# A convolution stack's two ends: W's first tile laid out whole, and a last layer with seven held tiles in four column tiles

## The chip, the cores and the metric

The kernel runs on one core of a Trainium2 chip. TensorE (PE in the profile, its weight loads PEld) multiplies matrices into PSUM; VectorE (DVE), ScalarE (ACT) and GpSimd (POOL) work on data in PSUM and SBUF; SyncE (SP) only issues DMAs. ScalarE and GpSimd issue DMAs too, each on a queue of its own. Each engine runs its instructions in the order written and waits on semaphores where it needs another's result. The metric is the device time of one execution in microseconds, and the profile shows one execution in detail.

## The reference, cut to what matters

The input x has 4 images of 32 x 32 pixels with 16 channels, in float32. Four layers follow each other, each with a residual: `x = x + layer(group_norm(x))`, with groups of two channels.

Layers 0 to 2 have this form, each with its own weights M, Wp and G:

```python
first = jnp.einsum('ijpq,bpqc->bijc', M2, inputs)
shifted = conv3x3(inputs, K)             # K is G: 32*32*16 output channels
shifted = shifted.reshape(b, h, w, h, w, f)
diff = jax.nn.relu(inputs[:, :, :, None, None, :] - shifted)
second = jnp.einsum('ijpq,bpqijc->bijc', W2, diff)
return first - second
```

For every one of the 1024 target positions there is a 3 x 3 convolution with its own weights over the whole image; its result is subtracted from the image, clipped at zero, and summed over the image with weights W.

Layer 3 is a convolution with the impulse response of a rational filter:

```python
H_truncated = jnp.fft.rfft2(b, s=(l1, l2)) / jnp.fft.rfft2(a, s=(l1, l2))
h_truncated = jnp.fft.irfft2(H_truncated, s=(l1, l2))
...
y = irfft2(einsum(rfft2(x), h0 + rfft2(h_truncated[0])))[..., :l1, :l2, :]
```

## The kernel before, in words

**Layers 0 to 2** (`conv_layer`). The 1024 positions are packed into 128 blocks of 8 positions x 16 channels, so that a block is 128 columns of weights. For one block and one of the four batches TensorE runs 12 matmuls (L470) into one PSUM pair: the taps lie in three weight tiles (`ga`, `gb`, `gn`) against three image copies `ims[a]`, one set for batches 0 and 1 (a = 0) and one for batches 2 and 3. VectorE then clips the result, multiplies it with a row of W and sums it, in one instruction (L478). Four PSUM pairs rotate, so TensorE can be at most four blocks ahead of VectorE.

G comes in chunks of 8 blocks (`load_g`), two 64-row loads each for `ga` and `gb` and one broadcast load for the last tap; `prepare_g` subtracts an identity on GpSimd (L398), casts on ScalarE (L402) and takes a remainder on VectorE (L405). W comes in tiles of two blocks, 1 MB each (`load_w`, L420): W's eight rows are each copied to 16 partitions, by a broadcast in the DMA. Six W tiles rotate, and a tile is fetched four tiles ahead of its use, on SyncE's queue. The first term is computed on the side (`first_term`): M's tiles (`load_m`) come from a pool `mp` of four buffers that is kept through the whole kernel.

**The start** loads three raw image copies for each half of the batches (`load_first`) and a first quarter of G's first chunk (`halves[0]`, two blocks) on three queues. The other three quarters (`halves[1]`) are loaded by GpSimd's queue. On SyncE's queue come, in this order, the copies for batches 0 and 1, the small G loads, two copies for batches 2 and 3, W's first tile in two halves (`load_w(2)`), W's second tile, and G's second chunk. `first_images` then normalises the copies: ScalarE subtracts the mean (L176), GpSimd clears borders (L194), ScalarE and VectorE scale (L180, L198 to L205).

**Steps on the side.** `step()` is called after every block and moves each generator in `todo` by one yield; this is how the norms are spread over the matmuls. `group_norm` yields once after the sums, once after the sums of squares are started, and once more, and only then has TensorE add the sums over the groups (L102).

**Layer 3.** While the earlier layers run, `impulse_response` writes the filter to DRAM (`hd`). `load_toeplitz` reads from it one tile of four rows of taps, with eight DMAs of 160 KB, half on SyncE's and half on ScalarE's queue. There are eight such tiles, used in the order 1, 7, 6, 5, 4, 3, 2, 0. Five are loaded during layer 2 into five buffers (`TB = 5`); the last three are loaded each into a buffer that layer 3 has just finished with. Tiles 1 and 0 are multiplied with 128 columns of the normalised image `y3` at a time. Tiles 7 to 2 are multiplied in groups of four matmuls with 32 columns each, a column tile for each, since a part of the output needs only some of the taps (`slots`). Results go to one PSUM bank for the part that lies in place (`po`) and three banks (`other`) for parts that belong to another block of rows. `po` shares a PSUM pair with `other[1]`, and `other[2]` with `other[3]`. VectorE adds the three banks to the residual `xo` at L722, after tiles 6, 4 and 2, and `po` at the end (L762). The residual itself is copied (L704), transposed on TensorE (L707) and copied back (L711) between the last norm and the first matmul of layer 3 (L747).

Of the kernel before, what the change touches and what calls it, by code (L numbers as in the profile page):

```python
# [37 lines left out]
P = 128  # L38
# [16 lines left out]
def conv_stack_kernel(ctx, tc, x, raw, M, W, G, den, num, h0, cst, dft, one, idp, idq, out):  # L55
# [10 lines left out]
    mp = ctx.enter_context(tc.tile_pool(name="mp", bufs=4))  # L66
# [233 lines left out]
    def load_m(layer, pm):  # L300
        mt = mp.tile([P, 2, 512], F32, tag="mt", name="mt")
        nc.sync.dma_start(out=mt.rearrange("k h n -> k (h n)"), in_=M[layer][:, pm])
        return mt

    def first_term(layer, xt):

        mts = [load_m(layer, 0)]
        yield
        py = small_psum()
        for b in range(B):  # L310
            nc.tensor.transpose(py[:, bass.ts(b, P)], yc[b // 2][:, b % 2, :], ident)  # L311
        yt = work.tile([P, 8, B, C], F32, tag="yt", name="yt")
        nc.vector.tensor_copy(yt, py.rearrange("k (b p c) -> k p b c", b=B, p=8))
        for pm in range(1, 4):
            mts.append(load_m(layer, pm))
            yield
        for _ in range(GC - 4):
            yield
        ft = work.tile([P, 2, 8, S], F32, tag="ft", name="ft")
        for part in range(2):  # L320
            pf = small_psum()
            for k in range(4):
                for h in range(2):
                    nc.tensor.matmul(  # L324
                        pf[64 * h : 64 * h + 64],
                        lhsT=yt[:, 4 * part + k].rearrange("k b c -> k (b c)"),
                        rhs=mts[k][:, h, :],
                        start=(k == 0),
                        stop=(k == 3),
                    )  # L330
            pv = pf.rearrange("k (cc p q) -> k cc p q", cc=2, p=8)
            if part == 0:
                nc.scalar.copy(ft, pv)
                mts = []
                for pm in range(4, 8):
                    yield
                    mts.append(load_m(layer, pm))
                for _ in range(GC - 4):
                    yield
            else:  # L340
                nc.vector.tensor_tensor(ft, ft, pv, ALU.add)  # L341
# [67 lines left out]
    def load_w(parts=1):  # L409
# [6 lines left out]
        src = W[layer][cc, :, q : q + 2, :].rearrange("p k m -> p (k m)")  # L416
        wts.append(wt)
        n = 2 * S * S // parts
        for k in range(parts):
            nc.sync.dma_start(  # L420
                out=wt.rearrange("p k m -> p (k m)")[:, bass.ts(k, n)],
                in_=src[:, bass.ts(k, n)].unsqueeze(1).to_broadcast([8, C, n]),
            )
            yield
# [10 lines left out]
    def conv_layer(layer, xt, finish, side=()):  # L435
# [15 lines left out]
        for job, (blks, batches) in enumerate(jobs):  # L451
            pairs = layer and job < 2, job >= len(jobs) - 2
            for k, blk in enumerate(blks):
                if any(pairs):

                    if k in ((4, 6) if job != len(jobs) - 2 else (0, 2)):
                        list(load_w())
                elif k % 2 == 0:
                    list(load_w())
                if k == (3 if job == 0 else 1):  # L460
                    list(load_g(layer, blk // GC + 1))
                if (job or not layer) and k == 6:
                    list(prepare_g(layer, blk // GC + 1))
                wt = wts[64 * layer + blk // 2][:, blk % 2, :]
# [163 lines left out]
    def load_toeplitz(k):  # L628

        t = tp.tile([P, TQ, C, PITCH], F32, tag="t", name="t")  # L630
        ts.append(t)
        n = TQ * C * PITCH
        for p in range(8):
            src = hd[8 + k * n - p :]
            (nc.sync, nc.scalar)[p % 2].dma_start(
                out=t[p * C : (p + 1) * C].rearrange("i q j r -> i (q j r)"),
# [221 lines left out]
```

## Time and profile before

| What | us |
|---|---|
| median of 3 runs | 3146.19 |
| lowest and highest | 3145.56, 3148.74 |
| profiled execution, its own time | 3146.99 |
| span of the profiled execution | 3145.2 |
| TensorE busy in it | 3112.3 |
| VectorE busy in it | 2069.8 |

All times in the profile are counted from the start of the span. Busy time of TensorE is modelled, since its matmuls overlap. One matmul of float32 is shown as two instructions, so that the 224 matmuls of layer 3 stand as 448. The profile's chain of waits runs back from the last instruction to whatever released it. "granted clock" is the share of TensorE's clock that a throttle let through; in this execution it was half for a part of the start (from 23.2 to 26.6 us) and from 3084.9 to 3095.2 us.

### The profile page before, as it was taken

How to read it: one execution, taken by the hardware profiler on the slowest of the kernel's cores; microseconds unless marked ns; L12 is line 12 of the kernel's file. 1: busy time of each engine (PE TensorE's matmuls, PEld its weight loads, DVE VectorE, ACT ScalarE, POOL GpSimd, SP SyncE). 2: the span in 40 equal slices, each digit the busy share in tenths (PEclk: the TensorE clock that was granted, in tenths of full speed). 3: DMA queues.
4: the chain of work that ended last, by engine and by line, in shares of the span. 5: the costliest groups of instructions: out<-in, count | busy, mean ns of one | idle time of the engine just before them, and what ended most of it. 6: DMA issues, size and time to landing. Idle time of an engine off the chain costs nothing.

```text
span 3145.2 us, 38886 instructions
## 1 busy us (share of the span) xinstructions
PE 3112.3 (99%) x16068; PEld 1563.7 (50%) x16068; DVE 2069.8 (66%) x3318; ACT 82.0 (3%) x107; POOL 235.1 (7%) x262
## 2 busy tenths in 40 slices
PE   7999999999999999999999999999999999999998
PEld 5545554454444554444444444455444444444444
DVE  6666766666667766666666666766666666666662
ACT  1000000000000000000000000000000000000000
POOL 2002320000000100100000000010010000000000
PEclk9999999999999999999999999999999999999999
DMA  7553344433443655433443344266544444444303
GB/s 193 133 129 93 88 108 110 99 88 88 96 99 71 132 142 124 98 88 88 98 97 87 88 98 97 61 137 150 127 101 98 97 114 103 98 99 111 88 14 54
DMA packets 67206, 321.18 MB, mean 102 GB/s; under 512 B 9987, under 2 KB 16901, under 8 KB 41557
## 3 DMA queue, kind: packets, MB, share of 16 engines
q1 hardware_dynamic: 56176, 299.31, 40.1%
q10 hardware_dynamic: 6356, 10.81, 1.8%
q0 software_dynamic: 4496, 8.58, 1.5%
q8 instruction: 126, 2.06, 0.3%
q14 instruction: 52, 0.42, 0.0%
HBM read 313.03 MB, written 5.63 MB: 101 GB/s over the span
## 4 chain that ended last, share of the span: by engine, by line
PE 98%; DMA 2%; DVE 1%; issue 0%; ACT 0%; SPq 0%; ACTq 0%; DVEq 0%
PE pt L470 95%; PE pt L747 1%; DMA t<-hd 1%; DMA w<-in_W_dram 1%; PE pt L324 1%; DVE junk L478 0%; DMA im<-in_raw_dram 0%; PE pt L523 0%; PE pt L566 0%; PE pt L102 0%; PE pt L605 0%; DVE x L493 0%; DVE s L111 0%; PE pt L311 0%; DVE xo L722 0%
## 5 line engine op out<-in xcount | busy, mean ns | idle before, releaser
L478 DVE SCALAR_TENSOR_TENSOR junk<-pt,w 128x1024 f32<-128x1024 f32 x1536 | 1880.8, 1224 | 999.5 <-PE pt L470 976.6
L470 PE MATMUL pt<-im,ga 64*128 64x512 f32 x6144 | 1592.3, 591 | 5.1 <-POOL im L194 2.8
L470 PE MATMUL pt<-im,gb 64*128 64x512 f32 x6144 | 1585.1, 589 | 3.5 <-ACT im L180 3.3
L470 PE MATMUL pt<-im,gn 64*128 64x512 f32 x3072 | 1259.8, 806 | 0.0
L470 PEld LDWEIGHTS pt<-im,gb 64*128 64x128 f32 x6144 | 607.0, 185 | 718.1 <-issue 707.7
L470 PEld LDWEIGHTS pt<-im,ga 64*128 64x128 f32 x6144 | 605.4, 187 | 435.2 <-DVE junk L478 278.0
L470 PEld LDWEIGHTS pt<-im,gn 64*128 64x128 f32 x3072 | 305.3, 186 | 356.6 <-issue 352.7
L398 POOL TENSOR_TENSOR ga<-ga,cs 128x1024 f32<-128x1024 f32 (+2 forms) x49 | 113.6, 2319 | 2129.3 <-DMA ga<-in_G_dram 2080.3
L478 DVE DVE_READ_ACCUMULATOR junk<-pt,w 128x1 f32 x1536 | 127.8, 83 | 0.0
L405 DVE TENSOR_TENSOR gn<-g,gn 32x1024 fp32r<-32x1024 f32 (+2 forms) x98 | 120.7, 1232 | 4.7 <-ACT gn L402 2.6
L402 ACT CAST gn<-g 128x1024 fp32r<-128x1024 f32 (+2 forms) x49 | 50.4, 1029 | 2332.1 <-DMA g<-in_G_dram 2201.0
L747 PE MATMUL pt<-t,y 128*32 128x512 f32 (+4 forms) x448 | 46.6, 440 | 4.8 <-DVE xo L722 2.7
L348 POOL DMA_DIRECT2D fd<-ft x48 | 25.1, 531 | 219.3 <-DVE ft L341 209.7
L747 PEld LDWEIGHTS pt<-t,y 128*32 128x32 f32 (+1 forms) x448 | 24.8, 125 | 26.7 <-issue 19.1
L722 DVE TENSOR_TENSOR xo<-xo,pt 32x512 f32<-32x512 f32 x5 | 3.4, 681 | 40.0 <-PE pt L747 39.9
L324 PE MATMUL pt<-mt,yt 128*64 128x512 f32 x96 | 21.9, 599 | 0.0
L291 POOL DMA_DIRECT2D im<-img x32 | 16.2, 515 | 9.1 <-DMA img<-y 9.1
L544 POOL TENSOR_TENSOR H<-H,d 128x256 f32<-128x256 f32 (+1 forms) x10 | 8.3, 826 | 68.1 <-DVE d L549 67.7
L324 PEld LDWEIGHTS pt<-mt,yt 128*64 128x64 f32 x96 | 6.4, 136 | 13.7 <-issue 9.4
L102 PE MATMUL pt<-s,cs 64*128 64x2 f32 (+1 forms) x28 | 2.9, 266 | 9.2 <-DVE s L111 9.2
L274 POOL COPY e<-y 32x612 f32<-32x612 f32 x4 | 2.8, 694 | 119.2 <-DVE y L273 119.2
L544 POOL TENSOR_TENSOR t<-s 128x256 f32<-128x256 f32 (+1 forms) x15 | 11.3, 756 | 0.0
(83 smaller groups left out, 186.3 us busy)
## 6 DMA issues: line engine op xcount, KB each, us to landing
w<-in_W_dram SPq DMA_DIRECT2D x191, 1024.0 KB
ga<-in_G_dram SPq DMA_DIRECT2D x94, 256.0 KB
gb<-in_G_dram SPq DMA_DIRECT2D x94, 256.0 KB
g<-in_G_dram SPq DMA_DIRECT2D x47, 512.0 KB
mt<-in_M_dram SPq DMA_DIRECT2D x24, 512.0 KB
t<-hd ACTq DMA_DIRECT2D x32, 160.0 KB
t<-hd SPq DMA_DIRECT2D x32, 160.0 KB
im<-img SPq DMA_DIRECT2D x32, 67.5 KB
```

Source lines behind the costliest of these rows:

```text
L102: nc.tensor.matmul(pt[:, h, : s.shape[1]], lhsT=avg[rows], rhs=s[rows], start=True, stop=True)
L291: (nc.sync, nc.scalar, nc.gpsimd)[n % 3].dma_start(out=ims[a][k][at : at + C] .bitcast(F32) .rearrange("c l b cc x -> c l (b cc x)")[:, :, ...
L324: nc.tensor.matmul(pf[64 * h : 64 * h + 64], lhsT=yt[:, 4 * part + k].rearrange("k b c -> k (b c)"), rhs=mts[k][:, h, :], start=(k == 0), ...
L348: nc.gpsimd.dma_start(out=fv[h, cc, b], in_=ft[at : at + C, cc])
L398: nc.gpsimd.tensor_tensor(gv, gv, mid.unsqueeze(1).to_broadcast([P, gv.shape[1], C]), ALU.subtract)
L402: nc.scalar.copy(gn, g9)
L405: nc.vector.tensor_tensor(lo, g9[r : r + 32], lo.bitcast(F32), ALU.subtract)
L470: nc.tensor.matmul(pt[:, half, :], lhsT=w[rows, blk % GC, :], rhs=im[rows, :, b % 2, :, :S], start=n == 0, stop=n == 2,)
L478: nc.vector.scalar_tensor_tensor(junk, pt.rearrange("p h m -> p (h m)"), 0.0, wt, ALU.min, ALU.mult, accum_out=acc[b // 2][:, b % 2, blk : ...
L544: mul = lambda o, u, w: nc.gpsimd.tensor_tensor(o, u, w, ALU.mult)
L722: nc.vector.tensor_tensor(out, out, src, ALU.add)
L747: nc.tensor.matmul(bank[cols].rearrange("n (j r) -> n j r", j=C)[:, :, 8 * cc :], lhsT=y3[:, cc, at : at + width, :].rearrange("p q b -> p ...
```

## The change

It touches both ends of the kernel.

At the start, W's first tile is laid out for all 128 partitions by the host (`w0`) and loaded with one plain DMA, instead of two broadcast DMAs. The load is issued ahead of the rest of G's first chunk, and the `ga` and `gb` loads of that rest move from GpSimd's queue to SyncE's, behind it. Its broadcast load for the last tap stays with GpSimd.

M's pool is opened inside `first_term` and closed after its last matmul, so that its space can be used later in each layer.

In layer 3, seven of the eight tiles are held when it starts: five as before, one in space that M's pool gave back (`tp2`), and one in the buffers of two W tiles that layer 2 no longer needs, loaded from its last job but one on (`late_toeplitz`). Only tile 0 is loaded during layer 3, into the buffer of tile 1. Tiles 1 and 0 are now also multiplied in four column tiles, and `po` has a PSUM pair of its own. VectorE's additions of the three other banks, one for each pair of column tile and block (five), all stand after the last tile but one. The residual's copy, transposes and copy back move into the norm of batches 2 and 3 (`norm3`, a = 1), between its two group sums. In doing so `norm3` takes two steps of `group_norm` itself and drops one of its yields, also for batches 0 and 1.

```diff
-    mp = ctx.enter_context(tc.tile_pool(name="mp", bufs=4))
...
     def first_term(layer, xt):
-        mts = [load_m(layer, 0)]
+        ft = work.tile([P, 2, 8, S], F32, tag="ft", name="ft")
+        with tc.tile_pool(name="mp", bufs=4) as mp:
+            mts = [load_m(mp, layer, 0)]
...
-    def load_w(parts=1):
+    def load_w():
...
+        nc.sync.dma_start(
+            out=wt.rearrange("p k m -> p (k m)"),
+            in_=src.unsqueeze(1).to_broadcast([8, C, 2 * S * S]) if wts else w0,
+        )
         wts.append(wt)
-        n = 2 * S * S // parts
-        for k in range(parts):
-            nc.sync.dma_start(
-                out=wt.rearrange("p k m -> p (k m)")[:, bass.ts(k, n)],
-                in_=src[:, bass.ts(k, n)].unsqueeze(1).to_broadcast([8, C, n]),
-            )
-            yield
...
+                if job == len(jobs) - 2:
+                    next(late, None)
...
-                (halves[1], nc.gpsimd, nc.gpsimd, nc.gpsimd),
+                (halves[1], nc.sync, nc.sync, nc.gpsimd),
...
+        load_w()
         list(loads)
-        list(load_w(2))
         first_images()
-        list(load_w())
+        load_w()
...
     def norm3(a, xt):
-        xc, rstd = yield from group_norm(xt[:, 2 * a : 2 * a + 2])
+        steps = group_norm(xt[:, 2 * a : 2 * a + 2])
+        if a:
+            xr = work.tile([P, 4, S, B], F32, tag="ft", name="xr")
+            nc.scalar.copy(xr, xt.rearrange("p b (cc q) -> p cc q b", q=S))
+        next(steps)
+        yield
+        next(steps)
+        if a:
+            px = small_psum()
+            for cc in range(4):
+                nc.tensor.transpose(
+                    px[:, bass.ts(cc, P)], xr[:, cc].rearrange("p q b -> p (q b)"), ident
+                )
+            nc.scalar.copy(xo, px.rearrange("n (r j) -> n r j", j=C))
+        xc, rstd = yield from steps
...
     def toeplitz():
         for k in order[:TB]:
-            for _ in load_toeplitz(k):
+            for _ in load_toeplitz(k, toeplitz_tile(tp)):
                 yield
                 yield
+        yield from load_toeplitz(order[TB], toeplitz_tile(ctx.enter_context(tc.tile_pool(name="tp2", bufs=1))))
+
+    def late_toeplitz():
+        half = TQ // 2 * C * PITCH
+        parts = []
+        for _ in range(2):
+            wt = wp.tile([P, 2, S * S], F32, tag="w", name="w").rearrange("p k m -> p (k m)")
+            parts.append(wt[:, :half].rearrange("p (q j r) -> p q j r", j=C, r=PITCH))
+        ts.append([part[:, q] for part in parts for q in range(TQ // 2)])
+        yield from load_toeplitz(order[TB + 1], *parts)
...
-    banks = [pair_psum(), pair_psum()]
-    po, other = banks[0][:, 0], {1: banks[0][:, 1], 2: banks[1][:, 0], 3: banks[1][:, 1]}
+    banks = [pair_psum() for _ in range(3)]
+    po, other = banks[0][:, 0], {1: banks[1][:, 0], 2: banks[1][:, 1], 3: banks[2][:, 0]}
...
-        [[(None, None, q)] for q in range(TQ)],
+        [[(t, t, q) for t in range(4)] for q in range(TQ)],
...
-        if n and n + TB - 1 < len(order):
-            list(load_toeplitz(order[n + TB - 1]))
+        if n == 1:
+            list(load_toeplitz(order[-1], toeplitz_tile(tp)))
...
-        if k == 6:
-            add(3, 2, other[3])
-        elif k == 4:
-            add(3, 1, other[3])
-        elif k == 2:
-            for block in range(1, 4):
-                add(block, 0, other[block])
+        if n == len(order) - 2:
+            for tile, block in sorted({m for m in every if m[0] != m[1]}):
+                row = xo[32 * block : 32 * block + 32]
+                src = other[block][32 * tile : 32 * tile + 32].rearrange("n (j r) -> n r j", j=C)
+                nc.vector.tensor_tensor(row, row, src, ALU.add)
...
+        if i == 0:
+            arrays["w0"] = np.repeat(arrays["W0"][0, :, :2].reshape(8, -1), C, axis=0)
```

## The prediction

> **What bounds the kernel now.** I read the page first: TensorE is busy almost all the time, and the chain of work that ended last is 95% convolution matmuls (L470).
>
> ```profile
> span 3145.2 us, 38886 instructions
> PE 3112.3 (99%) x16068; PEld 1563.7 (50%) x16068; DVE 2069.8 (66%) x3318; ACT 82.0 (3%) x107; POOL 235.1 (7%) x262
> PE pt L470 95%; PE pt L747 1%; DMA t<-hd 1%; DMA w<-in_W_dram 1%; PE pt L324 1%; DVE junk L478 0%; DMA im<-in_raw_dram 0%; PE pt L523 0%; PE pt L566 0%; PE pt L102 0%; PE pt L605 0%; DVE x L493 0%; DVE s L111 0%; PE pt L311 0%; DVE xo L722 0%
> ```
>
> Between about 30 and 3082 us a block (one position, one batch) costs TensorE 1.96 us (in the timeline one block's first matmul starts at 3077.81, the next one's at 3079.77) and VectorE 1.32 (1.23 + 0.08). The change leaves those instructions alone, so only the two ends can move. Second, the start, in the timeline and as windows (columns: window, its length, busy us of PE, PEld, DVE, ACT, POOL, then granted PE clock, DMA share, GB/s).
>
> ```profile
> 19.37 1.39 ACT L176 ACTIVATE im<-im,neg 128x544 f32<-128x544 f32 x2 [3.34 <-DMA im<-in_raw_dram]
> 22.30 1.39 ACT L180 ACTIVATE im<-im,rstd 128x544 f32<-128x544 f32 x2 [1.55 <-POOL im L194]
> 23.10 2.08 PE L470 MATMUL pt<-im,gb 64*128 64x512 f32 x4 [3.34 <-ACT im L180]
> 29.11 1.23 DVE L478 SCALAR_TENSOR_TENSOR junk<-pt,w 128x1024 f32<-128x1024 f32 x1 [7.11 <-DMA w<-in_W_dram]
> 30.40 1.13 PE L470 MATMUL pt<-im,ga 64*128 64x512 f32 x4 [2.30 <-DVE junk L478]
> ```
>
> ```profile
> 23.10:28.10 5.00, 4.99 (x16) 2.24 (x16) 0.00 (x0) 0.59 (x1) 1.80 (x1) 0.66 1.05 128
> 28.10:30.40 2.30, 0.00 (x1) 0.01 (x1) 1.23 (x2) 0.83 (x1) 0.00 (x0) 1.00 0.88 119
> 30.40:38.30 7.90, 7.90 (x40) 3.91 (x42) 7.34 (x12) 0.00 (x0) 0.00 (x0) 1.00 0.53 130
> ```
>
> TensorE fills its four PSUM buffers by 28.10 and then stands for 2.30 us, because VectorE cannot empty the first one before half of W's first tile lands at 29.1. One step earlier there is a second gate: batches 2 and 3 wait for the last image copy (landed 19.37), which goes through ScalarE, GpSimd and ScalarE again, and reaches TensorE 3.73 us later, at 23.10. Third, the end, as the chain (start, us, what) and in windows.
>
> ```profile
> 3089.00 1.12 PE pt L707 x4
> 3090.12 11.18 PE pt L747 x32
> ...
> 3114.65 9.15 DMA t<-hd
> 3123.80 0.18 issue
> 3123.98 6.70 PE pt L747 x96
> 3130.68 0.02 issue
> 3130.70 0.68 DVE xo L722
> 3131.38 0.03 issue
> 3131.41 0.69 DVE xo L722
> 3132.10 0.41 issue
> 3132.51 8.88 PE pt L747 x32
> ```
>
> ```profile
> 3106.59:3121.87 15.28, 15.28 (x224) 6.94 (x224) 0.68 (x1) 0.00 (x0) 0.00 (x0) 1.00 1.02 139
> ```
>
> **The change part by part: the start.** W's first tile (1 MB, in two halves) is now one plain 128-row load; the other 6/8 of G's first chunk (four loads of 192 KB) leave GpSimd's queue for SyncE's, behind that tile. (1) The W tile. The row for a broadcast tile is the last window of the start: 130 GB/s at a DMA share of 0.53, about 8 us per MB. The row for plain 128-row loads is the 5 to 10 us window, 321 GB/s: 1.05 MB / 321 = 3.3 us. Ends: 2.5 us (420 GB/s, the best 1.5 us slice of the first 60 us) and 8 us (if nothing is won). It sits on SyncE's queue directly behind the last image copy, so it lands near 19.0 + 3.3 = 22.3 us, at worst 27. (2) VectorE has image work in its order until 22.01, so the first L478 runs at about 22.3 instead of 29.11. (3) What is late next: the image copy, not W. Between 12 and 20 us GpSimd's queue moved 1.06 MB beside it (0.54 + 0.52 in the queue view), the rest of one image and G. The four G loads go away there, but the 384 KB broadcast of G's last taps, issued behind them, moves up and takes their place, so I give the copy 0.4 us only (ends: 1 us later, since broadcasts are the slow loads here, and 2.5 us earlier). TensorE then starts batch 2 at 22.7 and, with the 5.00 us that batches 2 and 3 took at a granted clock of 0.66, reaches the second block at 27.7 instead of 30.40: **-2.7 us**. The low end is -1.3 (copy 1 us later, 30.40 - 29.1). The high end is -5.5: copy 1.2 us earlier and the clock not dropped, so 3.3 us in place of 5.0.
>
> What is behind the moved loads: G's 768 KB at 269 GB/s (the 7.35 to 19.36 window) is 2.9 us, in by 25.2; GpSimd's subtraction (1.80) ends near 27 and TensorE needs it at 27.7 + 4 x 1.96 = 35.5. W's second tile stands behind them: 25.2 + 8 = 33.2, needed by VectorE at 37.5, and TensorE only stands if it is more than three blocks (5.9 us) later still. That cover is why the longer SyncE queue costs nothing; if the second tile took past 43 us, each us beyond is a us lost. GpSimd issues four DMAs fewer (about 0.54 each), which nothing on the path waits for. From there TensorE runs at 1.96 per block to the end, so the lead is kept.
>
> **The middle.** M's tiles now come from a pool opened per layer, whose space later tiles take over. The added waits are on M's readers (L324) and loads, which are over some blocks before: zero. The two more Toeplitz tiles (10 x 128 KB each, 2.6 MB) are loaded in layer 2 by SyncE and ScalarE: one between W tiles up to block 107 or so, one into the buffers of W tiles 58 and 59 after block 119. Queued behind them are the last W tiles, fetched four tiles (63 us) ahead, and ScalarE's cast of the last G chunk. DMA is idle from 2988 to 3066 us (share 0 in that slice of the page), and about 10 us per tile (9.60 and 9.15 in the chain) fits in the 63 us left: zero; ends 0 and +3 (one missed cast).
>
> The norm of batches 0 and 1 loses one step of delay: its second group sums stand one block earlier in TensorE's order. VectorE finishes ss at 3054.41, and sums follow VectorE by 0.14 (3084.12 to 3084.26); TensorE would be there at 3054.03, so it stands 0.5 us, with the restart **+0.6** (ends 0.4 and 0.9).
>
> **The end.** (a) The residual copy (1.08 on ScalarE) and four transposes (1.12) now run inside the last norm. x is ready at 3083.66, so the copy ends at 3084.8 and the transposes at 3085.95; the second sums wait for ss until 3086.42, so they hide, with 0.5 us to spare. The path is then y's end (3089.40) + 0.14: layer 3 starts at 3089.54, not 3090.12. (b) Seven tiles are held, so two of the three loads on the path go; the third is issued after the first tile, takes about 9.5 us, and has six tiles = 48 groups x 0.546 = 26 us of matmuls over it. (c) Tiles 1 and 0 change from 16 wide matmuls to 16 groups of four in column tiles. Rows: 15.28 us for 28 groups (224 instructions), 0.546 per group; wide, 8.88 / 16 = 0.555. So neutral. Ends 0.53 and 0.56. (d) The VectorE additions go to one place beside the last tile (5 x 0.68 = 3.4 under 8.8) and have PSUM tiles of their own, so TensorE's stalls of 0.86, 2.10 and 1.87 us at 3105.7, 3121.9 and 3130.7 all go (4.8 together).
>
> Sum: 80 groups x 0.546 = 43.7, plus the slow clock of the first tile, plus 0.2 to drain. The clock row: 0.77 over the 11.40 us from 3089.9, a loss of 2.6. 3089.54 + 46.5 = 3136.0; last addition at 3136.0 instead of 3141.42: **-5.4**. With +0.6: **-4.8** (ends -2.9 and -6).
>
> [...]
>
> Total -2.7 - 4.8 = -7.5 us. The profiled execution took 3146.99 (span 3145.2 and 1.8 around it), 0.8 above the median of 3146.19; its terms taken from the median give **3138.7 us**.
>
> **Rivals.**
> - A, as above: 3138.7, own range 3136 to 3141.5.
> - B, the start gives twice as much: copy 1 us earlier or the clock kept (for: 28 to 34 us show 1.00 once it is busy; against: TensorE would still be idle about 2.9 us from 19.8). -5.2 - 4.8: 3136.2.
> - C, one end gives little: the last-taps broadcast slows the image copy or W's tile by 2 us and more (for: 128 GB/s while broadcasts ran, from 23 to 28 us). 3141.4; with the end failing in its place, 3143.5.
> - D, slower: four column tiles that stream the very same rows from SBUF at once, as tiles 1 and 0 now do, take turns. In the trace groups share rows in pairs at most; pairs ran at 0.546 like the others, which speaks against it. 32 groups change, so the gain is gone at 0.546 + 7.5/32 = 0.78 us per group, slower by 0.2% at 0.98, and at full turns (2.18) the time is 3138.7 + 52 = 3191.
>
> **How the numbers follow.** A 0.59, B 0.15, C 0.18, D 0.08. A measurement of this kernel tells 0.2% (6.3 us) from no change, so the line is 3139.9. A lies below it three times in four (0.44), B always (0.15), C seldom (0.03): faster 0.62. The rest of A (0.15) and of C (0.15) is the same: 0.30. D is slower: 0.08. The range takes A, B and most of C: 3134.5 to 3143.
>
> **What would show it.** First L478 near 22 us with no wait for W of over 1 us, and block 1 starting near 27.7; the image copy still ending near 19. At the end, no wait for t or for xo from the second tile on, layer 3's matmuls in one run of about 46.5 us with 640 instructions, and all xo additions but one before it ends. Wrong would be: L478 waiting for W's second tile past 43 us, a group of tiles 1 or 0 above 0.6 us, a wait of ScalarE's last casts, or a granted clock below 0.77 for longer than the first tile.

## The result, and the profile after

The changed kernel took 3144.76 us (median of 3145.93, 3146.66, 3136.89 and 3143.59); the kernel before took 3147.06 in the runs beside it. The ratio is 0.9988, with a 95% interval from 0.997 to 1.0006: no difference that this measurement can tell. The forecast was 3138.7 and "faster". Both ends gave what was forecast, as the trace shows, and yet most of it is missing from the total. The profiled execution took 3145.93 with a span of 3144.1, which is 1.1 us below the span of before.

The page of the changed kernel: span, busy times, and the chain that ended last by line.

```profile
span 3144.1 us, 39279 instructions
PE 3113.4 (99%) x16260; PEld 1538.3 (49%) x16260; DVE 2070.0 (66%) x3318; ACT 81.8 (3%) x107; POOL 232.6 (7%) x258
PE pt L470 94%; PE pt L761 1%; DMA g<-in_G_dram 1%; DMA w<-in_W_dram 1%; PE pt L324 1%; DMA im<-in_raw_dram 0%; DVE junk L478 0%; PE pt L523 0%; PE pt L566 0%; PE pt L605 0%; PE pt L101 0%; DVE x L493 0%; DVE s L110 0%; PE pt L312 0%; DVE gn L405 0%
```

The loads of Toeplitz tiles (`t<-hd`) are gone from the chain, and of the additions to `xo` only the last one (0.69 us) is left on it, too short for this list. A load of G (`g<-in_G_dram`) and VectorE's remainder of G's last taps (`gn L405`) have come in. That is the first sign of where the gain went.

**The start.** The timeline of the changed kernel (start, us, engine, line, in brackets the wait before it):

```profile
19.15 1.39 ACT L175 ACTIVATE im<-im,neg 128x544 f32<-128x544 f32 x2 [3.04 <-DMA im<-in_raw_dram]
22.02 1.39 ACT L179 ACTIVATE im<-im,rstd 128x544 f32<-128x544 f32 x2 [1.48 <-POOL im L193]
22.82 1.21 PE L470 MATMUL pt<-im,gb 64*128 64x512 f32 x4 [2.95 <-ACT im L179]
24.25 1.22 DVE L478 SCALAR_TENSOR_TENSOR junk<-pt,w 128x1024 f32<-128x1024 f32 x1 [2.13 <-DMA w<-in_w_dram]
27.65 1.03 PE L470 MATMUL pt<-im,ga 64*128 64x512 f32 x4
```

W's first tile no longer holds TensorE up: the first L478, which still waits 2.13 us for it, runs at 24.25 in place of 29.11, and TensorE goes on to the second block at 27.65 without a gap, where it started at 30.40 before. (A block from here on is one block of weights with all four batches, 4 x 1.96 = 7.84 us of TensorE.)

**The middle.** Here is the loss. First the waits between 60 and 90 us in the changed kernel (who waited for whom: total, times, longest).

```profile
ACT gn L402 <- DMA g<-in_G_dram: 50.6, 1, 50.6
DVE gn L405 <- ACT gn L402: 7.5, 1, 7.5
PE pt L470 <- DVE junk L478: 4.6, 1, 4.6
```

Then its timeline at the same place:

```profile
74.74 1.04 ACT L402 CAST gn<-g 128x1024 fp32r<-128x1024 f32 x1 [50.61 <-DMA g<-in_G_dram]
75.81 2.45 DVE L405 TENSOR_TENSOR gn<-g,gn 32x1024 fp32r<-32x1024 f32 x2 [7.46 <-ACT gn L402]
```

And the same two instructions of the kernel before:

```profile
66.85 1.05 ACT L402 CAST gn<-g 128x1024 fp32r<-128x1024 f32 x1 [37.24 <-DMA g<-in_G_dram]
71.63 2.45 DVE L405 TENSOR_TENSOR gn<-g,gn 32x1024 fp32r<-32x1024 f32 x2
```

L405 stands in VectorE's order in front of the L478 that TensorE waits for. Before, its input was ready 3.7 us ahead of it. After, the last taps of G's second chunk land at 74.7, and VectorE stands for 7.46 us. TensorE fills its four PSUM buffers and stands too; windows of the changed kernel (length, then busy us of PE, PEld, DVE, ACT, POOL, the granted PE clock, DMA share, GB/s):

```profile
70.00:75.00 5.00, 4.94 (x26) 2.16 (x22) 0.00 (x0) 0.26 (x1) 0.00 (x0) 1.00 0.79 174
75.00:80.00 5.00, 0.42 (x2) 0.42 (x4) 4.04 (x5) 0.78 (x1) 0.00 (x0) 0.83 0.50 125
80.00:85.00 5.00, 5.00 (x14) 2.12 (x14) 4.50 (x8) 0.00 (x0) 0.00 (x0) 0.50 0.52 131
```

TensorE is busy for 0.42 of 5 us, and then runs at half clock until 85 us: a second charge for the same stall. The chain of the first 100 us says what the load waited for (start, us, what):

```profile
13.98 25.51 DMA w<-in_W_dram
...
39.57 35.14 DMA g<-in_G_dram
...
74.74 1.05 ACT gn L402
...
75.81 0.07 DVE gn L405
```

The load is issued at 39.57, behind W's third, fourth and fifth tile on SyncE's queue, and lands 35.14 us later:

```profile
26.63 3.36 SPq L417 DMA_DIRECT2D w<-in_W_dram  x3
39.57 0.60 SPq L380 DMA_DIRECT2D g<-in_G_dram  x1
```

In the kernel before it stood behind the same three tiles, was issued 3.2 us later and landed some 24 us after that:

```profile
42.73 0.60 SPq L380 DMA_DIRECT2D g<-in_G_dram  x1
```

Those tiles moved at different rates in the two profiled executions, though the DMAs are the same. First the window of before, then that of after:

```profile
50.00:65.00 15.00, 15.00 (x80) 12.82 (x78) 9.16 (x16) 0.00 (x0) 0.00 (x0) 1.00 0.51 201
```

```profile
50.00:65.00 15.00, 15.00 (x80) 7.50 (x78) 9.32 (x16) 0.00 (x0) 0.00 (x0) 1.00 0.52 121
```

The DMA engines are just as occupied (0.51 and 0.52), but move 201 GB/s in the one and 121 in the other.

**The end.** The chain of the changed kernel:

```profile
3091.03 0.43 DVE ss L126
...
3093.64 0.62 DVE y L701
3094.26 0.14 issue
3094.39 45.64 PE pt L761 x640
3140.03 0.02 issue
3140.06 0.69 DVE xo L775
```

The timeline with the work that was moved into the last norm, and behind it the windows of layer 3:

```profile
3088.78 1.07 ACT L689 COPY xr<-x 128x512 f32<-128x512 f32 x1 [28.08 <-DVE x L493]
3089.90 0.66 PE L696 MATMUL pt<-cs,xr 128*128 128x128 f32 x4 [0.22 <-ACT xr L689]
```

```profile
3094.39:3106.00 11.61, 11.61 (x136) 5.23 (x140) 0.00 (x0) 0.00 (x0) 0.00 (x0) 0.80 0.01 1
3106.00:3120.00 14.00, 14.00 (x209) 6.58 (x205) 0.00 (x0) 0.00 (x0) 0.00 (x0) 1.00 0.67 96
3120.00:3140.06 20.06, 19.99 (x304) 9.52 (x296) 3.41 (x6) 0.00 (x0) 0.00 (x0) 1.00 0.01 2
```

Layer 3 is one run of 640 instructions that waits for no tile and no addition; the transposes end 0.9 us before `ss` is ready. Its last tile, tile 0, which used to be wide, in the timeline:

```profile
3131.19 8.80 PE L761 MATMUL pt<-t,y 128*32 128x512 f32 x128
```

The two spans, cut at four points (us):

| stretch | before | after | difference |
|---|---|---|---|
| start to the second block's first matmul | 30.40 | 27.65 | -2.75 |
| from there to block 8's (the first of G's second chunk) | 55.23 | 62.62 | +7.4 |
| from there to the start of the last L478 | 2996.3 | 2996.7 | +0.4 |
| last x (L493) to the end of the span | 61.97 | 55.87 | -6.1 |

The four differences add up to -1.1, the difference of the spans (the 1.3 us between the third and the fourth stretch are the same in both).

### The profile page after: what moved, and what is told of

It is laid out like the page before. It is cut to its first block, busy times and chain, and to the rows that moved or that the text cites. A ratio compares the mean times of both kernels' runs of the same rounds, so it can differ in the third digit from the quotient of the medians.

```text
span 3144.1 us, 39279 instructions
## 1 busy us (share of the span) xinstructions
PE 3113.4 (99%) x16260; PEld 1538.3 (49%) x16260; DVE 2070.0 (66%) x3318; ACT 81.8 (3%) x107; POOL 232.6 (7%) x258
## 4 chain that ended last, share of the span: by engine, by line
PE 97%; DMA 2%; DVE 1%; issue 0%; SPq 0%; ACT 0%; DVEq 0%
PE pt L470 94%; PE pt L761 1%; DMA g<-in_G_dram 1%; DMA w<-in_W_dram 1%; PE pt L324 1%; DMA im<-in_raw_dram 0%; DVE junk L478 0%; PE pt L523 0%; PE pt L566 0%; PE pt L605 0%; PE pt L101 0%; DVE x L493 0%; DVE s L110 0%; PE pt L312 0%; DVE gn L405 0%
## 5 line engine op out<-in xcount | busy, mean ns | idle before, releaser
L478 DVE SCALAR_TENSOR_TENSOR junk<-pt,w 128x1024 f32<-128x1024 f32 x1536 | 1881.1, 1225 | 996.8 <-PE pt L470 979.9
L470 PEld LDWEIGHTS pt<-im,gb 64*128 64x128 f32 x6144 | 596.1, 186 | 730.6 <-issue 724.2
L405 DVE TENSOR_TENSOR gn<-g,gn 32x1024 fp32r<-32x1024 f32 (+2 forms) x98 | 120.7, 1231 | 12.4 <-ACT gn L402 10.2
L478 DVE DVE_READ_ACCUMULATOR junk<-pt,w 128x1 f32 x1536 | 128.0, 83 | 0.0
L402 ACT CAST gn<-g 128x1024 fp32r<-128x1024 f32 (+2 forms) x49 | 50.4, 1028 | 2357.7 <-DMA g<-in_G_dram 2133.7
L761 PE MATMUL pt<-t,y 128*32 128x128 f32 (+3 forms) x544 | 39.3, 452 | 2.4 <-DVE y L701 2.4
L761 PEld LDWEIGHTS pt<-t,y 128*32 128x32 f32 x544 | 18.3, 114 | 23.1 <-issue 20.5
L324 PEld LDWEIGHTS pt<-mt,yt 128*64 128x64 f32 x96 | 6.4, 136 | 13.7 <-issue 9.7
```

Source lines behind the costliest of these rows:

```text
L324: nc.tensor.matmul(pf[64 * h : 64 * h + 64], lhsT=yt[:, 4 * part + k].rearrange("k b c -> k (b c)"), rhs=mts[k][:, h, :], start=(k == 0), ...
L402: nc.scalar.copy(gn, g9)
L405: nc.vector.tensor_tensor(lo, g9[r : r + 32], lo.bitcast(F32), ALU.subtract)
L470: nc.tensor.matmul(pt[:, half, :], lhsT=w[rows, blk % GC, :], rhs=im[rows, :, b % 2, :, :S], start=n == 0, stop=n == 2,)
L478: nc.vector.scalar_tensor_tensor(junk, pt.rearrange("p h m -> p (h m)"), 0.0, wt, ALU.min, ALU.mult, accum_out=acc[b // 2][:, b % 2, blk : ...
L761: nc.tensor.matmul(bank[32 * tile : 32 * tile + 32] .rearrange("n (j r) -> n j r", j=C)[:, :, 8 * cc :], lhsT=y3[:, cc, at : at + 8, :].re ...
```

## The experiments

The theory to be tested: the load of the second chunk's last taps is late because it stands behind W's tiles in SyncE's queue, and the whole loss in the middle is VectorE's wait for it. The rivals: the earlier start itself brings the loss (more transfers at once, a throttle); the end gave less than its trace shows (the "layer-3 theory"); or the broadcast loads happened to be slow in that execution, whatever the order (the "slow-reads theory"). For each run the median, the range and the number of executions are given, and the ratio to the kernel before in the same session. That kernel's medians were 3145.94 (s1 to s4), 3147.23 (s5, s7, s8, s9) and 3146.02 (s6, s10, s11, s12).

### s1: the new start alone

The kernel before, with `w0` and the new queue order and the end as it was.

```diff
-                (halves[1], nc.gpsimd, nc.gpsimd, nc.gpsimd),
+                (halves[1], nc.sync, nc.sync, nc.gpsimd),
...
+        load_w()
         list(loads)
-        list(load_w(2))
         first_images()
...
```

(`load_w` itself as in the change.)

> Only the start's part of the change (W's first tile laid out whole, G's rest behind it on SyncE's queue); layer 3, M's pool and the norm as before. Taps theory (VectorE stands at L405 because the second chunk's last taps land late behind the longer SyncE queue): block 1 starts near 27.7 us instead of 30.4, L405 of the second chunk waits for its cast 5 us or more near 68 to 76 us, TensorE stands 4 to 5 us there and has a half clock after it; the time is 2 to 6 us above before, near 3151. Layer-3 theory (the loss comes from M's pool, the late tiles or the norm): no such wait, and 2.7 us below before, near 3143.5. Slow-reads theory (the broadcast loads happened to be slow in that execution, whatever the order): the wait comes and goes, with a mean near 3147.

Measured: 3146.53 (3141.01 to 3150.05, 11), ratio 0.9997 [0.9988, 1.0005]. In its trace the second block starts at 26.36, but L405 waits 6.90 us for the cast at 72.89, and from there to block 8 it takes 61.9 us. The start's gain is there and is paid back in the middle, with no change at the end of the kernel needed for that, so the layer-3 theory falls. The size was missed: the taps theory gave 3151, and the median is 0.6 us above before; the slow-reads theory's "comes and goes, with a mean near 3147" fits better.

### s2: the new end alone

The changed kernel with the start as before (the lines above, the other way round).

> Only the rest of the change (M's pool per layer, seven held tiles, four column tiles, the residual inside the norm); the start as before. Taps theory: the end gives 5 to 6 us and nothing is lost in between, near 3141.5, with last taps of the second chunk landing before VectorE wants them near 71.6. Layer-3 theory: the loss of 7 to 8 us shows here, near 3149. Slow-reads theory: 3141 in executions with fast broadcasts and up to 8 us more in others.

Measured: 3142.74 (3139.88 to 3148.21, 11), ratio 0.9987 [0.9978, 0.9995]. It is 3.2 us below before, less than the 6.1 that the trace of the changed kernel shows at the end: here too L405 waits, 4.47 us, at 75.05. So the old start also loses time at this place in some executions. The kernel before had no wait there in its profiled execution, the one that the forecast was read from. The taps theory had expected none here either.

### s3: the changed kernel with the second chunk's last taps loaded early

One move: the load is issued ahead of W's third tile, not behind W's fifth.

```diff
-        loads = load_g(0, 1)
-        next(loads)
+        list(load_g(0, 1))
         load_w()
         load_w()
-        todo.append(loads)
```

> The changed kernel with one load moved: the last-tap broadcast of G's second chunk is issued right behind that chunk's other loads, ahead of W's third and fourth tiles instead of behind W's fifth. Taps theory: they land near 50 us, L405 near 68 us has no wait, TensorE runs through, and the time is 3136.5 to 3138.5. Layer-3 theory: no change from the changed kernel, near 3144.8. Slow-reads theory: W's third and fourth tiles are now late in their place, and the time stays within 2 us of 3144.8.

Measured: 3138.77 (3136.89 to 3139.81, 9), ratio 0.9974 [0.9965, 0.9983]. The cast in the timeline of s3, and a window of it:

```profile
47.43 1.05 ACT L402 CAST gn<-g 128x1024 fp32r<-128x1024 f32 x1 [23.41 <-DMA g<-in_G_dram]
```

```profile
70.00:80.00 10.00, 10.00 (x56) 4.83 (x52) 8.10 (x13) 0.00 (x0) 0.00 (x0) 1.00 0.63 169
```

The cast is done 20 us before L405 is due (68.31, no wait), TensorE has no gap, and the second block to block 8 takes 54.97 us. This is the forecast's time to 0.1 us, from the kernel without the wait. The bands of the two other theories start from the result's 3144.8, which the unaltered kernel, measured beside this one, did not reach either (s4), so the time alone does not decide against them; the trace does, with no wait and no loss.

### s4: the changed kernel again

> The changed kernel once more, unaltered, for a second profile and more times. Taps theory: times fall in two groups, near 3137 where the second chunk's last taps land before about 68 us, and near 3145 to 3146 where they land after 74; the new profile shows the wait of L405 and the time that go together. Layer-3 theory: one group near 3145, whatever L405 waits. Slow-reads theory: as the taps theory, with packets of W's tiles near 0.31 us where it is fast and near 0.57 where it is slow.

Measured: 3139.06 (3136.97 to 3146.31, 12), ratio 0.9977 [0.9968, 0.9985]. Nine of the twelve lie between 3136.97 and 3139.41, the others at 3141.23, 3143.08 and 3146.31. Its profiled execution (3139.41) shows a wait of 4.60 us at L405, of which TensorE feels 1.8, and no half clock there. The two groups of times that were expected (near 3137 and near 3145 to 3146) do not show. Together with the four executions of the result, sixteen of this kernel have a median of 3139.2, and five lie above 3143. So the loss is not a constant: most executions take about 3139, and three of the four of the result are among those five. Against s3 in the same session the medians differ by only 0.3 us; what s3 lacks is the upper tail (its highest is 3139.81). Of the five above 3143 only one has a trace, that of the result; that the other four lost their time at the same place is not shown.

### s5: the kernel before with the same move

```diff
-        loads = load_g(0, 1)
-        next(loads)
+        list(load_g(0, 1))
         list(load_w())
         list(load_w())
-        todo.append(loads)
```

> The kernel before with one load moved: the last-tap broadcast of G's second chunk goes ahead of W's third and fourth tiles. Taps theory: L405 near 71.6 us has no wait, TensorE runs through between 60 and 90 us; most executions of before have only a small wait there (0 to 3 us), so the median moves by 1 us at most, 3145 to 3146.5, but none is above 3149, where before had six of 33 above 3151. Rival (the wait at L405 belongs to the new start alone): spread and median both as before.

Measured: 3146.26 (3143.79 to 3149.66, 11), ratio 0.9996 [0.9987, 1.0005]. TensorE is busy for all of 60 to 90 us. Its profiled execution was its slowest (3149.66, where none above 3149 was expected), with 3.6 us of TensorE standing until 29.17, for W's first tile, and a half clock between 28 and 35 us, so the start varies for reasons of its own. Inconclusive: the move alone is worth between -4 and +1.6 us for the kernel before.

### s7 and s8: each end alone, with the same move

s7 is s1 with the move of s3; s8 is s2 with it.

> The start's part of the change alone, with that load moved. Taps theory: the start's 2.7 us now reach the end, 3143 with a narrow spread of some 3 us, against 3146.5 and a spread of 9 us for the start's part without the move. Rival (the start gives nothing that lasts): 3145.5 to 3146.5, as the kernel before with the load moved.

> The rest of the change alone (M's pool, seven held tiles, column tiles, residual in the norm), with that load moved. Taps theory: 4.8 us below the kernel before with the load moved, near 3141, narrow; together with the start's 2.7 that gives the 3138.8 of the whole change with the load moved. Rival (the parts do not add): below 3139.5 or above 3143.

Measured: s7 3142.21 (3139.12 to 3143.39, 11), 0.9985 [0.9976, 0.9994]; s8 3140.53 (3139.85 to 3143.97, 11), 0.9979 [0.997, 0.9988]. Both medians are within 0.8 us of the taps theory's, and neither rival's is met. In both traces L405 finds its cast done, begun at 47.33 and 50.92. Against s5 in the same session the start is worth 4.0 us and the end 5.7. Without the move the start alone was worth nothing (s1). Together that is 9.7, where s3 was 7.2 below before (s12, the same kernel in another session, 8.6). The uncertainty of a sum of such differences is some 3 us, and the half-clock pieces at both ends fall differently from trace to trace (at the end 10.2 us of half clock before and 6.8 after). How much of the rest is real stays open.

### s9: the first chunk's last taps out of the image copy's way

The forecast let the broadcast of the first chunk's remaining last taps share the DMA engines with the last image copy. Here it is issued by GpSimd after the images have been normalised.

```diff
         load_w()
-        list(loads)
+        next(loads)
         first_images()
+        list(loads)
```

(made on s3)

> The changed kernel with the second chunk's last-tap load moved as before, and besides the last-tap broadcast of the rest of the first chunk issued by GpSimd behind its image clears (near 20 us) instead of near 3 us. If that broadcast is what holds the last image copy back, as the prediction has it, the copy lands near 17 us instead of 19.1, block 1 starts 1.5 to 2 us earlier than 27.6, and the time is near 3137. If bandwidth of the rest holds it, the copy stays near 19 and the time within 0.7 us of 3138.8. If the broadcast in its new place delays W's second tile, VectorE waits for that tile near 36 us and the time is 1 us or more above 3138.8.

Measured: 3142.68 (3141.6 to 3143.64, 11), ratio 0.9985 [0.9976, 0.9994], 4.6 us below before, where s3 was 7.2 below in its own session: a net loss of some 2.6. The second block does start 3.4 us earlier than in s3, at 24.15; half of that is the half clock, which s3's trace has there and this one has not, so that 1.7 us are the copy's (TensorE's second batches start at 20.98 in place of 22.71). But now the first chunk's cast is late:

```profile
36.91 0.83 ACT L402 CAST gn<-g 128x768 fp32r<-128x768 f32 x1 [15.35 <-DMA g<-in_G_dram]
37.78 1.93 DVE L405 TENSOR_TENSOR gn<-g,gn 32x768 fp32r<-32x768 f32 x2 [6.22 <-ACT gn L402]
38.78 0.79 PE L470 MATMUL pt<-im,gn 64*128 64x512 f32 x1 [4.90 <-DVE gn L405]
```

The same wait one chunk earlier, on the same two lines, with a half clock from 38.4 to 45.2 behind it. The broadcast did hold the image copy back, and moving it too far costs more than that. The loss that was expected for a bad place was a wait for W's second tile; the wait that came is another.

### s6: the dose

The changed kernel with the load of the second chunk's last taps behind five W tiles in place of three.

```diff
-        todo.append(loads)
+        def later():
+            for _ in range(16):
+                yield
+            yield from loads
+        todo.append(later())
```

> The changed kernel with one thing moved: the load of the second chunk's last taps is issued behind two more of W's tiles (the sixth and seventh) on SyncE's queue, so behind five in place of three. If that load's place in the queue is the cause (taps theory): in the changed kernel's first profile it landed at 74.7 us and VectorE stood at L405 for 7.5 us. Two more tiles of 1 MB at 115 to 210 GB/s take 10 to 18 us, so VectorE stands at L405 some 10 to 25 us, TensorE has three blocks (5.9 us) of cover, and the time is 10 to 22 us above the kernel with the load moved early (3138 to 3143): 3149 to 3163. If the stand of VectorE costs nothing in time (rival: the loss in the middle is the throttle's or the chip's, whatever VectorE waits for): within 3 us of the changed kernel's 3139 to 3145.

Measured: 3148.69 (3146.36 to 3159.98, 12), ratio 1.0013 [1.0003, 1.0023], 11.2 us above s12 of the same session. The median falls between the two bands, 0.3 us under the theory's and 0.7 above the rival's; against the kernel with the early load it is inside the 10 to 22 that the theory gave. The trace decides. The waits from 60 to 110 us in s6, and a window of it:

```profile
DVE gn L405 <- ACT gn L402: 16.5, 1, 16.5
...
PE pt L470 <- DVE junk L478: 13.7, 1, 13.7
```

```profile
76.00:93.10 17.10, 6.03 (x16) 2.76 (x18) 8.60 (x12) 1.04 (x1) 0.00 (x0) 0.51 0.45 186
```

TensorE stands for 13.7 us and then works at half clock up to 93 us; VectorE's wait is more than twice that of the changed kernel's profile, with nothing but this load moved. This execution took 3153.66, 17.0 us more than the profiled one of s12, and 16.6 of them lie between the second block and block 8.

### s12: s3 again

> The kernel of s3 unaltered (the second chunk's last taps loaded ahead of W's third tile), as the measure for the other three. If s3's result was the kernel and not that chip's hour: 5 to 9 us below the kernel before, within 1.5 us above and below its median, no wait at the second chunk's L405, TensorE without a gap from 60 to 90 us.

Measured: 3137.46 (3136.67 to 3139.5, 8), ratio 0.9972 [0.9962, 0.9982]. The seventeen executions of this kernel in two sessions span 3.1 us, the sixteen of the changed kernel 9.8. In its trace the second block starts at 25.89, as no half clock falls there; in s3's it did, and it was 27.57. L405 has no wait and TensorE no gap from 60 to 90 us, as expected. The early load has a price on VectorE: L478 waits 5.18 us for W's third tile at 56.06 (3.33 in s3, and 1.9 at most in the traces without the move), which TensorE's PSUM buffers cover.

### s10: s3 with the step given back to the norm of batches 0 and 1

```diff
             nc.scalar.copy(xo, px.rearrange("n (r j) -> n r j", j=C))
+        else:
+            yield
         xc, rstd = yield from steps
```

> The changed kernel with the second chunk's last taps loaded early, and the dropped yield given back to the norm of batches 0 and 1 alone. Theory: that norm's second group sums stand one block later in TensorE's order and TensorE no longer waits for VectorE's sums of squares near 3055 us, which is worth 0.6 to 0.8 us against the kernel with the early load alone (s12 of the same call), too little for the interval to tell but visible in the trace as a wait that is gone. Rival: the step is needed for what follows (the copy of the residual or y comes later), and the kernel is 0 to 2 us slower than s12.

Measured: 3138.27 (3136.42 to 3138.69, 6), ratio 0.997 [0.9959, 0.9981]. The second group sums in s10 and then in s12:

```profile
3049.23 0.42 DVE L126 TENSOR_REDUCE ss<-sq 128x2 f32<-128x256 f32 x1
...
3051.23 0.31 PE L101 MATMUL pt<-ss,cs 64*128 64x2 f32 x4
```

```profile
3049.45 0.42 DVE L126 TENSOR_REDUCE ss<-sq 128x2 f32<-128x256 f32 x1
...
3050.02 0.39 PE L101 MATMUL pt<-ss,cs 64*128 64x2 f32 x4 [0.32 <-DVE ss L126]
```

With the step, the sums stand a block later and wait for nothing; from block 8 to the last L478 s10 takes 2996.14 us and s12 2997.03, 0.9 less, where 0.6 to 0.8 was expected. Part of that is chance: the nine traces with s12's norm take 2996.55 to 2997.23 (mean 2996.76), the four with the old end 2995.96 to 2996.55 (mean 2996.21). The time does not show it: s10's trace then has 10.2 us of half clock at the end and s12's 6.8, and the medians differ by 0.8 the other way. Seen in the trace, inconclusive in the time.

### s11: s9's broadcast in a better place

On s3: the first chunk's remaining last taps go to SyncE's queue, behind `w0` and that chunk's other loads, and ahead of W's second tile.

```diff
-                (halves[1], nc.sync, nc.sync, nc.gpsimd),
+                (halves[1], nc.sync, nc.sync, nc.sync),
```

> The changed kernel with the second chunk's last taps loaded early, and with the broadcast load of the first chunk's other last taps put on SyncE's queue behind that chunk's other loads, in place of GpSimd's. Theory from s9: without that broadcast beside it the last image copy lands 2 to 3.4 us earlier, block 1 starts at 24 to 25.5 us in place of 27.6. The load then lands near 25 + 3 = 28 us, its cast and remainder are over by 31, and block 2 needs them at 24.2 + 4 x 1.96 = 32: no wait, and 1.5 to 3 us below s12. Rival: it lands after 31 us as in s9 (or W's second tile, now behind it, lands after 41 us); TensorE waits 2 to 6 us and may lose another 3 at half clock: 1 to 5 us above s12.

Measured: 3135.11 (3134.33 to 3135.84, 5), ratio 0.9961 [0.9949, 0.9974]; it beats both kernels, and all of its executions lie below the lowest of s12 (3136.67). From the timeline of s11, and then two of its windows:

```profile
14.65 2.65 ACT L175 ACTIVATE im<-im,neg 128x544 f32<-128x544 f32 x4
27.42 0.83 ACT L402 CAST gn<-g 128x768 fp32r<-128x768 f32 x1 [6.21 <-DMA g<-in_G_dram]
31.23 1.93 DVE L405 TENSOR_TENSOR gn<-g,gn 32x768 fp32r<-32x768 f32 x2
36.76 1.23 DVE L478 SCALAR_TENSOR_TENSOR junk<-pt,w 128x1024 f32<-128x1024 f32 x1 [2.00 <-DMA w<-in_W_dram]
...
54.71 1.23 DVE L478 SCALAR_TENSOR_TENSOR junk<-pt,w 128x1024 f32<-128x1024 f32 x1 [5.91 <-DMA w<-in_W_dram]
```

```profile
22.00:34.00 12.00, 12.00 (x62) 5.85 (x62) 11.28 (x18) 0.83 (x1) 2.07 (x3) 1.00 0.69 123
34.00:46.00 12.00, 12.00 (x64) 5.86 (x62) 8.81 (x17) 0.12 (x1) 2.37 (x1) 1.00 0.53 119
```

ScalarE no longer waits for the last image copy (both copies in one row at 14.65), the second block starts at 23.80, and the broadcast lands at 27.4, 3.8 us before L405 comes to it. VectorE waits 2.00 us for W's second tile, and TensorE's PSUM buffers cover it. Then it waits 5.91 us for W's third, which both moved loads now precede, and here the cover is used up: TensorE stands for 0.62 us.

## Why the prediction was wrong

**The step that failed** is "From there TensorE runs at 1.96 per block to the end, so the lead is kept": from the second block to block 8 that is 28 x 1.96 = 54.9 us, and the changed kernel took 62.62. The step rests on the sentence "That cover is why the longer SyncE queue costs nothing". It was worked out for two of the things queued behind the moved loads, GpSimd's subtraction and W's second tile. Both held: the subtraction was in time (over at 30.2; the forecast needed it at 35.5), and W's second tile, which landed at 39.5 and not 33.2, stayed within the 43 us that the prediction allowed. The list missed the last item of the queue at the start: the second chunk's last taps, behind W's third to fifth tile. The description of the start has the same gap: it names G's second chunk as one item behind W's second tile, but its last taps are a load of their own, three tiles later.

The longer queue did not itself make that load late in the profiled execution: it was issued 3.2 us earlier than before. It was late because the three tiles ahead of it moved more slowly. And it was needed earlier: its reader on VectorE, L405, stands in front of the blocks in VectorE's order, and the earlier start brings it forward (68.3 in place of 71.6). In that stretch no matmul waits for this load by name; the chain from the load to TensorE runs over ScalarE and VectorE. The traces, ordered by when the last taps' cast began:

| kernel | cast L402 at | L405 waits | second block to block 8 |
|---|---|---|---|
| s3 | 47.4 | 0 | 54.97 |
| before | 66.9 | 0 | 55.23 |
| s4 | 71.7 | 4.6 | 57.03 |
| s1 | 72.9 | 6.9 | 61.94 |
| s2 (old start) | 74.0 | 4.5 | 57.85 |
| after | 74.7 | 7.5 | 62.62 |
| s6 | 82.2 | 16.5 | 71.76 |

Without the wait this stretch takes 55 us (s7, s8, s10 and s12, with the early load too, 54.97 to 55.55). The exception is s5: no wait, but 57.78, as the half clock that follows its stand at the start lies in the stretch. Up to 4.6 us of wait cost 2 to 3, as the PSUM buffers cover the first part (TensorE stood 1.8 us in s4); from 6.9 on TensorE stands for 4.1 us or more, a half clock follows, and about the whole wait is lost.

s3 and s6 move only that load. Behind two more tiles the median rises by 11.2 us against s12. Ahead of the tiles the wait is gone from every trace and the upper tail from the times (the highest falls from 3146.31 in s4 to 3139.81), while the median hardly moves (0.3 us). The rival that the earlier start is itself the cause falls with s7 (the new start, load early: no loss in the middle); its part is that L405 comes sooner. Slow reads alone are not the cause either: in s12 the tiles moved at 125 GB/s from 50 to 65 us, about as slowly as the changed kernel's 121, and nothing was lost.

**Why the profile of before did not warn.** There the cast ended 3.7 us ahead of L405. That margin came from an execution in which W's tiles moved at 201 GB/s between 50 and 65 us; with the 121 GB/s of the changed kernel's profile, three tiles of 1 MB take 26 us in place of 16, and the margin is gone. In the same stretch the thirteen other traces moved 121 to 165 GB/s: the profile that the forecast was read from was the fast exception. s2, with the old start, shows the wait in the kernel's old order. What sets the rate in an execution no run here tells: the tile's packets (8 KB each) took about 0.31 us in one stretch and 0.57 in another of the same trace (before: 65 to 85 us and 1400 to 2000 us), and the stretches lie elsewhere in each. The prediction took 3.7 us for a property of the kernel; it was one draw, and a lucky one.

**The other steps.** The second block was given 27.7 and came at 27.65; TensorE's second batches 22.7 and 22.82; the image copy about 19 and 19.15. W's first tile landed at 24.2, not 22.3: it came 1.9 us later than said, within the 27 given as the worst, and without cost to TensorE, which had until 27.65, though VectorE waited 2.13 us for it, where no wait of over 1 us was forecast. The copy did gate the start, as the prediction put it, and s11 shows the price of the broadcast that took the moved loads' place beside it: about 2 us against s12, where the prediction gave it between "1 us later" and "2.5 us earlier" and took almost nothing. Its end of -5.5 for the start was reckoned with a copy 1.2 us earlier, not with these 2.5; s11 came to -6.6 (23.80). Rival B's -5.2 needs both of its conditions, though it says "or": from 22.7 and 27.7 a copy 1 us earlier gives -3.7 and the clock kept -4.4, and s12, where the clock stayed at 1.00, came to -4.5 (25.89). The gain of 2.75 is also on the high side: 30.40 was a late start of the old kernel, and the other traces with the old start have the second block at 28.9 to 29.2.

The norm of batches 0 and 1 was given as 0.6; 0.9 (s12 against s10) and 0.55 (the means above) stand on either side. The end gave 6.1, given as 5.4: layer 3 took 45.64 us, not 46.5, and nothing in it waited. The 640 instructions, a granted clock of 0.80 over the first 11.6 us included, average 0.57 us per group of eight (a matmul in each of the four column tiles). Tile 0 alone, at full clock, took 8.80 us for its 16 groups, 0.55 each, where its wide form took 8.88, so rival D (column tiles that take turns) falls.

**The sum.** -2.7 + 0.6 - 5.4 = -7.5 against -2.75 + 0.4 - 6.1 = -8.5 for the same terms in the trace; what is missing is one term of +7.4 that was priced at zero. None of the rivals named it: C had the same sign, but the wrong transfers. Most executions of the changed kernel (median of sixteen 3139.2) and all of s3 and s12 lie near the predicted 3138.7. The prediction left out not a change of the typical time but a wait that comes in part of the executions, and so the range of four. That three of the result's four executions lie above 3143, against two of the next twelve, was bad luck as far as these sixteen can tell; the wait that makes such a time possible was not.

## What to carry to other kernels

When a transfer is moved in a queue, follow every load behind it to its reader, through the engines in between, down to the end of the queue; the one that fails may be the smallest and two engines away from the bound. A margin of a few us read from one profiled execution is no margin where it rests on transfers whose rate varies between executions: bound it by the slowest rate that the trace shows anywhere for the same DMA. A small load that is needed soon goes ahead of the large ones: here that took the spread from 9.8 to 3.1 us (s3 and s12), and placing one more broadcast by the same rule gave the fastest kernel (s11, 3135.11, five executions). It is not free: what it overtakes comes later, and VectorE's wait for W's third tile grew from at most 1.9 us to between 2.5 and 5.9 (s9 aside), just inside the cover of TensorE's PSUM buffers, and in s11 0.62 us beyond it.

## What the runs showed of the hardware

The same broadcast load of 1 MB ran at 201 GB/s or 121 GB/s (before and after, 50 to 65 us) with nearly the same DMA share (0.51 and 0.52), in stretches that differ from execution to execution. Why the share stayed near a half, no run here shows.

TensorE's longer stalls had a second price. Half clock came in pieces of 3.4 us (23.2 to 26.6 before, 23.7 to 27.1 in the changed kernel), 6.8 us (78.4 to 85.2 in the changed kernel, 38.4 to 45.2 in s9), 10.2 us (from 3084.9 on, before) and 17.1 us (from 75.8 on, in s6), and where they fall differs between executions of the same kernel: one was at the second block in s3 and none in s12, which moved it by 1.7 us. Between 18 and 100 us, six stands (3.34 us before, 3.59 in s5, 4.09 in s1, 4.64 in the changed kernel, 4.90 in s9 and 13.71 in s6) each brought a half clock, and the 2.30 before and the 1.79 in s4 did not. Of four in between, 2.95 in the changed kernel and 2.75 in s3 did, and 2.7 in s6 and 2.55 in s12 did not. In the changed kernel 4.6 us of standing became 7.4 us of time.
